# A list scheduler's cost model rewritten: turns at SBUF, durations by form, tiling changes, and new stage targets

## The chip, the cores and the metric

The kernel runs on one core of one Trainium2 chip, in one launch. The metric is device time in microseconds (us); the time before is the median of three runs. The engines are TensorE (PE, with its weight loads as PEld), VectorE (DVE), ScalarE (ACT), GpSimd (POOL) and SyncE (SP), which issues the transfers.

## The reference

The input is 32 images of 56 x 56 pixels and 96 channels, in fp32. Four layers follow each other on each image.

```python
# layer 0: conditional block. rw: four expert weights per image
rw = sigmoid(mean(x, (1, 2)) @ Wr + br)
h = relu(bn1(x @ einsum("be,ecm->bcm", rw, Wpw) + rw @ bpw))     # 96 -> 384 channels
h = relu(bn2(sum_e rw[e] * (depthwise3x3(h, Wdw[e]) + bdw[e])))
x = bn3(h @ einsum("be,emf->bmf", rw, Wpwl) + rw @ bpwl) + x     # 384 -> 96
# layer 1: x + depthwise5x5(x, kernel)
# layer 2: bn(pointwise(depthwise3x3(relu(x))))
# layer 3: shifted-window attention (7 x 7 windows, 3 heads of 32), then an MLP 96 -> 384 -> 96 with gelu,
#          layer norms ahead of both, residuals around both
```

## The kernel before, in words

The work of an image is four stages, written as Python generators. **stage_router** brings the image in as xT (96 channels by 3136 pixels), averages it on ScalarE, and mixes the experts' weights on VectorE (wmix, wmix2, mix and biases). **stage_conditional** goes through 4 strips of 14 rows by 3 blocks of 128 channels: `expand` makes h1 by a matmul and a ScalarE activation with a border of one pixel; then nine taps of the depthwise filter run over h1, the first on ScalarE, the other eight as scalar_tensor_tensor on VectorE (128 x 784 elements, output h2); `project` brings 384 channels back to 96 (y), and GpSimd adds y into xT. That makes 96 such VectorE instructions an image, 3072 in all. **stage_depthwise** does both depthwise layers as 32x32 matmuls with banded weights (band, twelve to a group, sixteen tiles of TensorE side by side), moves results by DMA (x1, x3, filtered), and makes the tokens by `filtered x pw` into res. **stage_swin** normalizes (`normalized`: square on ScalarE, sum on VectorE into var, power -0.5 and multiplication on GpSimd into lnd), turns lnd by a TensorE transpose into slots or hT, makes queries, keys and values (wq, wk, wv), scores (kT x qT), exponentials on ScalarE (exps; GpSimd masks some), denominators and averages (ones32, v), the projection wo, and the MLP (`hidden`: w1 and gelu into hid; `perceptron`: w2, and tb summed by GpSimd and VectorE and stored).

Buffers are rings of a few slots: eight PSUM banks for everything, one h1 for each of the three channel blocks, three lnd, two tb, two image buffers xT, five hid, two hT.

No instruction is issued when a stage calls it. A `Recorder` notes every call with its reads and writes and a target time; `order()` then runs a list scheduler over all notes, with a clock of its own, and `give()` issues the calls in the order found. Therefore all instructions have one line in the profile, L500, and are told apart by their tiles. Calls under `together()` stay one unit. On the chip each engine works through its instructions in that fixed order and waits on semaphores; the scheduler's clock has no part in it.

The list scheduler works as follows. Each unit has a duration from `cost()` (L165, with the table COST, L146), and a target from its stage: image number plus a start, plus a share of a length, both from PLAN (L157). Each engine has a queue sorted by target. Whenever an engine is free on the scheduler's clock, it begins the first unit in its queue whose inputs are ready and whose buffers are free. A result counts as ready for TensorE only after TO_TENSOR (L160), for another engine after CROSSING (L158); DMAs land after LANDING. A GpSimd unit and a VectorE scalar_tensor_tensor that overlap are both slowed by SHARING = 1.36. If TensorE has had nothing that it could begin for SPARE_AFTER (L161), the scheduler puts in a spare matmul of ident by ident (128x128) into a free bank. These fillers are real instructions of the program.

The recorded calls go out here:

```python
for w in self.order():
    ...
    for method, args, kw in w.calls:
        ...
        getattr(getattr(self.nc, w.engine), method)(*args, **kw)
```

A second version of the kernel for large attention scores is in the program under a branch, and is not run with this input.

Of the kernel before, what the change touches and what calls it, by code (L numbers as in the profile page):

```python
# [23 lines left out]
P = 128  # L24
# [83 lines left out]
def tile_scores_in_range(ctx: ExitStack, tc: tile.TileContext, a: dict, flag: bass.AP):  # L108
# [35 lines left out]


COST = {  # L146
    ("vector", "scalar_tensor_tensor"): (150, 1.16), ("vector", "tensor_tensor"): (180, 0.96),
    ("vector", "tensor_scalar"): (190, 0.78), ("vector", "tensor_reduce"): (180, 0.95),
    ("vector", "tensor_copy"): (180, 1.1), ("vector", "reciprocal"): (180, 6.2),
    ("scalar", "activation"): (200, 0.72), ("scalar", "copy"): (200, 0.72),  # L150
    ("gpsimd", "tensor_tensor"): (200, 2.1), ("gpsimd", "memset"): (150, 0),
    ("sync", "dma_start"): (550, 0),
}
LANDING = 3000
IMAGE_LANDING = 12000

PLAN = {"router": (-0.14, 1), "conditional": (0.72, 1.14), "depthwise": (1.48, 1.13), "swin": (3.09, 0.92)}  # L157
CROSSING = 350  # L158

TO_TENSOR = {"vector": 1500, "gpsimd": 1500, "scalar": 1000, "sync": 700}  # L160
SPARE_AFTER = 250  # L161
SHARING = 1.36


def cost(engine, method, args, kw):  # L165
    if method == "preload_act_table_set":
        return 1300
    out = kw["out"] if "out" in kw else args[0]
    n = math.prod(out.shape[1:])
    if engine == "tensor":  # L170
        if method == "transpose":
            return 127
        k, m = args[1].shape[0], math.prod(args[1].shape[1:])
        if k == 32 and m == 32:
            return 68 * n / 392
        if k == 32:
            return 86
        if m == 32:
            return 75 if n < 128 else 255
        return 195 if n < 128 else 80 + 1.6 * n  # L180
    if len(args) > 3 and args[3] == ALU.pow:
        return 200 + 200 * n
    fixed, each = COST[engine, method]
    if engine == "scalar":
        if kw.get("accum_out") is not None:
            fixed += 190
        if hasattr(kw.get("scale"), "shape"):
            each += 0.37 if hasattr(kw.get("bias"), "shape") else 0.23
        elif hasattr(kw.get("bias"), "shape"):
            each += 0.25  # L190
    return fixed + each * n


# [67 lines left out]
class Recorder:  # L261
# [30 lines left out]
    def call(self, engine, method, args, kw, reads=(), writes=()):  # L292
# [46 lines left out]
    def order(self):  # L339
# [15 lines left out]
        for w in self.work:  # L355
            for b in w.uses:
                b.left = len(b.users)
        queues = {e: [] for e in self.ENGINES}
# [16 lines left out]
        running = {}  # L375

        def share(now):

            nonlocal count
            rate = SHARING if len(running) > 1 else 1.0  # L380
            for r in running.values():
                r["left"] -= (now - r["since"]) / r["rate"]
                r["since"], r["rate"] = now, rate
                r["end"] = free[r["work"].engine] = now + max(r["left"], 0.0) * rate
                heapq.heappush(events, (r["end"], count, r))
                count += 1
# [16 lines left out]
        now = 0.0  # L403
        count = 0

        def begin(w):
            nonlocal count
            for b in w.needs:
                if b.slot is None:
                    b.ring.free.sort()  # L410
                    b.slot = b.ring.free.pop(0)[1]
                    b.ring.begun += 1
            result.append(w)
            w.start = now
# [12 lines left out]

        left = len(self.work)
        spares = 0
        begun = False  # L430
        while left:
            for e in self.ENGINES:
                if free[e] > now:
                    continue
                held = []
                while queues[e]:
                    item = heapq.heappop(queues[e])
                    w = self.work[item[1]]
                    if not available(w):
                        held.append(item)  # L440
                        continue
                    begin(w)
                    left -= 1
                    if e == "tensor":
                        spares, begun = 0, True
                    break
                else:
                    if e == "tensor" and begun and self.spare and now >= free[e] + SPARE_AFTER and self.spare[2].free:
                        lhs, rhs, ring = self.spare
                        w = Work(e, 0.0)  # L450
                        b = Buffer(ring)
                        operands = View(b, ring.tiles[0])[:, : rhs.shape[1]], lhs, rhs
                        w.calls.append(("matmul", operands, {"start": True, "stop": True}))
                        w.ns = cost(e, "matmul", operands, {})
                        w.needs, w.starts, w.uses, w.writes = [b], [b], [b], [b]
                        b.users[w], b.left, b.owner = True, 1, w
                        spares += 1
                        assert spares < 10000, "no work can start"
                        begin(w)
                for item in held:  # L460
                    heapq.heappush(queues[e], item)
            assert events, "no work can start"
            now = events[0][0]
            ready = []
            while events and events[0][0] <= now:
                _, _, w = heapq.heappop(events)
                if isinstance(w, tuple):
                    put(w[0])
                elif isinstance(w, dict):

                    if w["end"] == now and running.get(w["work"].engine) is w:
                        del running[w["work"].engine]
                        w["work"].end = now
                        done(w["work"], now)
                        share(now)
# [28 lines left out]
def kernel(  # L504
# [994 lines left out]
    def when(stage, b):  # L1499

        start, length = PLAN[stage]
        return b + start, length
# [64 lines left out]
```

## Time and profile before

| | us |
|---|---|
| median of three runs | 5206.15 |
| lowest and highest | 5203.51, 5209.27 |
| span of the profiled execution | 5212.6 |
| TensorE busy | 5050.6 |
| VectorE busy | 4300.9 |
| ScalarE busy | 3836.9 |
| GpSimd busy | 3028.8 |

The profiled execution has no time of its own beside its span, which is 6.45 us (0.12%) above the median of the runs. The page names the engines PE, PEld, DVE, ACT, POOL and SP. Its groups show a tile with what it is made from: `h<-h,mix,h` are the taps on VectorE, `banks<-x,band` the 32x32 matmuls, `banks<-ident` the fillers (1672 records, two for each fp32 matmul), `lnd<-res,var` GpSimd's multiplication in the layer norms. Mean durations of the main groups: taps 1113 ns, GpSimd's addition into xT 1838 ns, its power into var 1519 ns, its multiplication into lnd 1168 ns, gelu 582 ns. A line of waits names the waiting engine and tile, what it waited for, the sum in us, how often, and the longest. [...] The profiled core ran at a mean granted TensorE clock of 0.985.

### The profile page before, as it was taken

To read this page: it belongs to the slowest core of one execution; us is meant where nothing else is said; L and a number is where in the kernel's file an instruction comes from. 1 tells how busy PE (TensorE), PEld (TensorE's weight loads), DVE (VectorE), ACT (ScalarE), POOL (GpSimd) and SP (SyncE) were. 2 spreads that over 40 slices of the span, in tenths; PEclk is the share of its full clock that TensorE was granted. 3 is DMA by queue.
4 is the path that set the end of the run, shared out by engine and by line. 5 is a ranking of instruction groups with operands and counts; after the bars stand their busy time and mean duration, and the time that the engine had idled before them with its cause. 6 is when DMAs were issued, how large, how long until landed. Compare 5 with 4: busy or idle time off the path is not lost.

```text
span 5212.6 us, 139630 instructions
## 1 busy us (share of the span) xinstructions
PE 5050.6 (97%) x58578; PEld 3343.9 (64%) x58578; DVE 4300.9 (83%) x5561; ACT 3836.9 (74%) x7649; POOL 3028.8 (58%) x2432
## 2 busy tenths in 40 slices
PE   5789999999999999999999999999999999999999
PEld 4556666666666666666666666666666666666677
DVE  7877988888888888888888888888888888888722
ACT  3457778877778777777877777877777877777755
POOL 5455766565665556666555665656576555566533
PEclk9899999999999999999999999999999999999999
DMA  1111101111111111111111111111111111110110
GB/s 43 23 28 37 38 18 32 33 39 36 39 21 30 31 39 36 39 23 30 33 35 37 37 30 26 30 36 38 37 35 22 32 33 39 36 39 21 23 28 19
DMA packets 482577, 166.34 MB, mean 32 GB/s; under 512 B 477951, under 2 KB 478612, under 8 KB 478868
## 3 DMA queue, kind: packets, MB, share of 16 engines
q1 hardware_dynamic: 481940, 157.33, 14.8%
q8 instruction: 463, 7.59, 0.6%
q14 instruction: 174, 1.43, 0.1%
HBM read 41.60 MB, written 38.54 MB: 15 GB/s over the span
## 4 chain that ended last, share of the span: by engine, by line
PE 74%; POOL 10%; DVE 5%; ACT 5%; issue 4%; DMA 1%; SPq 0%; ACTq 0%; DVEq 0%; POOLq 0%
PE banks L500 74%; DVE h L500 3%; POOL tb L500 3%; POOL lnd L500 2%; POOL xT L500 2%; ACT exps L500 2%; POOL exps L500 2%; POOL var L500 1%; ACT hid L500 1%; ACT h L500 1%; DMA out<-tb 1%; DVE wmix L500 1%; DVE hid L500 1%; ACT slots L500 0%; DVE res L500 0%
## 5 line engine op out<-in xcount | busy, mean ns | idle before, releaser
L500 DVE SCALAR_TENSOR_TENSOR h<-h,mix,h 128x784 f32<-128x784 f32 x3072 | 3309.6, 1113 | 71.1 <-ACT h L500 54.0
L500 POOL TENSOR_TENSOR var<-var,mhalf 112x4 f32<-112x4 f32 (+1 forms) x512 | 775.2, 1519 | 426.3 <-DVE var L500 419.6
L500 PE MATMUL banks<-x,band 32*32 32x392 f32 x24576 | 856.3, 510 | 0.0
L500 POOL TENSOR_TENSOR xT<-y,xT 96x392 f32<-96x392 f32 x256 | 470.2, 1838 | 445.5 <-ACT y L500 444.1
L500 PE MATMUL banks<-xT,wmix 96*128 96x448 f32 (+1 forms) x1536 | 697.9, 553 | 0.5 <-DVE wmix L500 0.5
L500 ACT ACTIVATE h<-h,biasd,s 128x784 f32<-128x784 f32 x384 | 398.9, 1039 | 366.1 <-DVE h L500 366.0
L500 ACT ACTIVATE hid<-banks,c 128x448 f32<-128x448 f32 (+1 forms) x768 | 436.5, 582 | 288.3 <-PE banks L500 279.9
L500 POOL TENSOR_TENSOR tb<-res 112x384 f32<-112x384 f32 (+1 forms) x256 | 476.4, 1866 | 286.7 <-DMA out<-tb 196.7
L500 PEld LDWEIGHTS banks<-w,hid 128*112 128x112 f32 x5376 | 584.7, 183 | 82.0 <-issue 37.8
L500 PE MATMUL banks<-hT,w 96*128 96x448 f32 (+1 forms) x1536 | 615.6, 502 | 0.2 <-DVE tb L500 0.2
L500 POOL TENSOR_TENSOR lnd<-res,var 112x384 f32<-112x384 f32 (+1 forms) x512 | 594.8, 1168 | 32.8 <-PE banks L500 16.2
L500 ACT ACTIVATE h<-banks,bias,s 128x448 f32<-128x448 f32 (+1 forms) x768 | 538.6, 709 | 91.0 <-PE banks L500 85.4
L500 PE MATMUL banks<-w,hid 128*112 128x96 f32 x5376 | 593.1, 267 | 7.4 <-ACT hid L500 6.4
L500 PE MATMUL banks<-h,wmix 128*96 128x392 f32 x1536 | 557.7, 501 | 15.7 <-ACT h L500 15.7
L500 PEld LDWEIGHTS banks<-x,band 32*32 32x32 f32 x24576 | 404.7, 103 | 250.9 <-issue 165.9
L500 ACT ACTIVATE exps<-banks 49x196 f32<-49x196 f32 x1536 | 506.2, 330 | 40.2 <-PE banks L500 15.3
L500 POOL TENSOR_TENSOR exps<-exps,keep_column 49x147 f32<-49x147 f32 x224 | 207.1, 925 | 480.8 <-ACT exps L500 427.4
L500 PEld LDWEIGHTS banks<-h,wmix 128*96 128x96 f32 x1536 | 244.1, 165 | 256.8 <-issue 209.2
L500 PEld LDWEIGHTS banks<-xT,wmix 96*128 96x128 f32 x1536 | 261.2, 192 | 200.7 <-issue 95.5
L500 DVE TENSOR_REDUCE var<-lnsq 112x4 f32<-112x388 f32 (+1 forms) x512 | 253.1, 497 | 157.6 <-POOL lnd L500 118.1
L500 ACT ACTIVATE h<-h,mix 128x784 f32<-128x784 f32 x384 | 364.5, 949 | 18.0 <-POOL h L500 10.1
L500 PEld LDWEIGHTS banks<-hT,w 96*128 96x128 f32 x1536 | 256.4, 190 | 144.9 <-issue 74.8
(132 smaller groups left out, 7460.2 us busy)
## 6 DMA issues: line engine op xcount, KB each, us to landing
xT<-in_x SPq DMA_DIRECT2D x32, 1176.0 KB
x<-xT SPq DMA_DIRECT2D x384, 98.0 KB
out<-tb SPq DMA_DIRECT2D x128, 168.0 KB
filtered<-x SPq DMA_DIRECT2D x384, 49.0 KB
filtered<-x SPq DMA_DIRECT2D x384, 42.0 KB
out<-tb SPq DMA_DIRECT2D x128, 126.0 KB
filtered<-x SPq DMA_DIRECT2D x384, 7.0 KB
wpw<-in_L_conv_Wpw SPq DMA_DIRECT2D x1, 576.0 KB
```

Of the source, the lines that this page charges most:

```text
L500: getattr(getattr(self.nc, w.engine), method)(*args, **kw)
```

## The change

Only the scheduler's model and its constants change; the stages and what they compute stay as they are.

- **Durations.** COST gets new values for nearly every form. VectorE's tensor_reduce is priced by its input, not its output. GpSimd's tensor_tensor goes from 200 + 2.1 n to 230 + 1.5 n ns for n elements, its power from 200 + 200 n to 370 + 160 n. A DMA issue takes SP 120 instead of 550 ns.
- **TensorE.** `tensor_time()` prices a unit by its columns and by how many tiles work side by side. A unit whose `tiling()` (rows and columns rounded up to 32, 64 or 128) differs from the one before costs CHANGE = 170 ns more. Code to prefer units of the same tiling is added, and switched off by SAME = 0.
- **Turns at SBUF.** Instead of slowing both by 1.36, a tensor_tensor or scalar_tensor_tensor of VectorE or GpSimd that touches no PSUM holds a single port for its whole duration (`in_memory`, `port`); the next one begins after it, in the order in which the scheduler reached them.
- **AHEAD.** An engine takes its next unit 37 to 100 ns before the end of the last.
- **Latencies and fillers.** CROSSING 350 to 522; TO_TENSOR lower for every engine; SPARE_AFTER 250 to 459.
- **Targets.** PLAN is set anew: the router starts 0.36 of an image earlier, the depthwise stage 0.05 later and shorter; the conditional stage is nearly and the attention stage exactly as before.
- **available()** refuses a unit that uses a buffer which has no slot yet and which another unit begins.

```diff
 COST = {
...
-    ("gpsimd", "tensor_tensor"): (200, 2.1), ("gpsimd", "memset"): (150, 0),
-    ("sync", "dma_start"): (550, 0),
+    ("vector", "scalar_tensor_tensor"): (155, 1.11), ("vector", "tensor_tensor"): (150, 1.02),
+    ("vector", "tensor_scalar"): (150, 1.04), ("vector", "tensor_reduce"): (145, 1.02),
...
+    ("gpsimd", "tensor_tensor"): (230, 1.5), ("gpsimd", "memset"): (145, 0),
+    ("sync", "dma_start"): (120, 0),
 }
+AHEAD = {"vector": 77, "scalar": 100, "gpsimd": 37, "tensor": 0, "sync": 0}
...
-PLAN = {"router": (-0.14, 1), "conditional": (0.72, 1.14), "depthwise": (1.48, 1.13), "swin": (3.09, 0.92)}
-CROSSING = 350
-
-TO_TENSOR = {"vector": 1500, "gpsimd": 1500, "scalar": 1000, "sync": 700}
-SPARE_AFTER = 250
-SHARING = 1.36
+PLAN = {"router": (-0.499, 0.953), "conditional": (0.712, 1.141), "depthwise": (1.529, 1.103), "swin": (3.09, 0.92)}
+CROSSING = 522
+
+TO_TENSOR = {"vector": 1155, "gpsimd": 1362, "scalar": 778, "sync": 136}
+SPARE_AFTER = 459
+CHANGE = 170
+SAME = 0
+
+def up(n):
+    return 32 if n <= 32 else 64 if n <= 64 else 128
+
+def tiling(call):
+    return tuple(up(n) for n in call[1][1].shape[:1] + (math.prod(call[1][1].shape[1:]),))
+
+def tensor_time(calls):
+    rows, columns = tiling(calls[0])
+    beside = min(len(calls), (P // rows) * (P // columns))
+    if beside == 16 and len(calls) % 16:
+        beside = 12
+    total = 30 if beside > 1 else 0
+    for method, args, kw in calls:
+        m = math.prod(args[1].shape[1:])
+        n = args[1].shape[0] if method == "transpose" else math.prod(args[2].shape[1:])
+        total += 2 * ((max(n, m) if beside == 1 else n) / 1.2 + 5) / beside
+    return total
+
+def in_memory(w):
+    method, args, kw = w.calls[0]
+    return method in ("tensor_tensor", "scalar_tensor_tensor") and not any(
+        isinstance(v, View) and v.buffer.ring.banks for v in args
+    )
...
         def available(w):
+            if any(b.slot is None and b.owner is not w and b not in w.needs for b in w.uses):
+                return False
...
-            if e == "gpsimd" or e == "vector" and w.calls[0][0] == "scalar_tensor_tensor":
-                running[e] = {"work": w, "left": w.ns, "since": now, "rate": 1.0}
-                share(now)
-                return
-            free[e] = now + w.ns
+            ns = w.ns
+            if e == "tensor":
+                if w.tiling != last[0]:
+                    ns += CHANGE
+                last[0] = w.tiling
+            begun_at = now
+            if w.in_memory:
+                begun_at = max(now, port[0])
+                port[0] = begun_at + ns
+            free[e] = begun_at + ns - AHEAD[e]
             heapq.heappush(events, (free[e], count, None))
-            heapq.heappush(events, (free[e] + w.landing, count + 1, w))
+            heapq.heappush(events, (begun_at + ns + w.landing, count + 1, w))
```

More of the change, by code (lines that the diff above doesn't have):

```diff
@@ L146 @@
 COST = {
[L147 to L150, printed above, removed]
-    ("gpsimd", "tensor_tensor"): (200, 2.1), ("gpsimd", "memset"): (150, 0),
-    ("sync", "dma_start"): (550, 0),
+    ("vector", "scalar_tensor_tensor"): (155, 1.11), ("vector", "tensor_tensor"): (150, 1.02),
@@ L153 @@
+    ("vector", "tensor_scalar"): (150, 1.04), ("vector", "tensor_reduce"): (145, 1.02),
+    ("vector", "tensor_copy"): (150, 1.04), ("vector", "reciprocal"): (150, 6.2),
+    ("scalar", "activation"): (210, 0.72), ("scalar", "copy"): (210, 0.7),
+    ("gpsimd", "tensor_tensor"): (230, 1.5), ("gpsimd", "memset"): (145, 0),
+    ("sync", "dma_start"): (120, 0),
 }
+AHEAD = {"vector": 77, "scalar": 100, "gpsimd": 37, "tensor": 0, "sync": 0}
 LANDING = 3000
 IMAGE_LANDING = 12000
-PLAN = {"router": (-0.14, 1), "conditional": (0.72, 1.14), "depthwise": (1.48, 1.13), "swin": (3.09, 0.92)}
@@ L165, in cost @@
 def cost(engine, method, args, kw):
+    if engine == "tensor":
+        return 0
     if method == "preload_act_table_set":
@@ L169, in cost @@
     n = math.prod(out.shape[1:])
[L170 to L180, printed above, removed]
     if len(args) > 3 and args[3] == ALU.pow:
-        return 200 + 200 * n
+        return 370 + 160 * n
     fixed, each = COST[engine, method]
+    if method == "tensor_reduce":
+        n = math.prod(args[1].shape[1:])
     if engine == "scalar":
@@ L187, in cost @@
         if hasattr(kw.get("scale"), "shape"):
-            each += 0.37 if hasattr(kw.get("bias"), "shape") else 0.23
+            each += 0.32 if hasattr(kw.get("bias"), "shape") else 0.21
         elif hasattr(kw.get("bias"), "shape"):
-            each += 0.25
+            each += 0.2
     return fixed + each * n
@@ L357, in order @@
                 b.left = len(b.users)
+            w.in_memory = w.engine in ("vector", "gpsimd") and in_memory(w)
+            if w.engine == "tensor":
+                w.tiling, w.ns = tiling(w.calls[0]), tensor_time(w.calls)
+        port, last = [0.0], [None]
         queues = {e: [] for e in self.ENGINES}
@@ L373, in available @@
             )
[L375 to L386, printed above, removed]
         def done(w, now):
@@ L435, in order @@
                 held = []
+                first = None
                 while queues[e]:
@@ L441, in order @@
                         continue
+                    if e == "tensor" and SAME:
+                        if first is None:
+                            first = item
+                        if item[0] > first[0] + SAME:
+                            held.append(item)
+                            w = None
+                        elif w.tiling != last[0]:
+                            held.append(item)
+                            continue
+                        if w is None:
+                            break
                     begin(w)
@@ L445, in order @@
                         spares, begun = 0, True
+                    first = None
                     break
-                else:
+                if first is not None:
+                    held.remove(first)
+                    begin(self.work[first[1]])
+                    left -= 1
+                    spares, begun = 0, True
+                elif free[e] <= now:
                     if e == "tensor" and begun and self.spare and now >= free[e] + SPARE_AFTER and self.spare[2].free:
@@ L453, in order @@
                         w.calls.append(("matmul", operands, {"start": True, "stop": True}))
-                        w.ns = cost(e, "matmul", operands, {})
+                        w.tiling, w.ns = tiling(w.calls[0]), tensor_time(w.calls)
+                        w.in_memory = False
                         w.needs, w.starts, w.uses, w.writes = [b], [b], [b], [b]
@@ L468, in order @@
                     put(w[0])
[L469 to L475, printed above, removed]
                 elif w is not None:
```

## The prediction

> **What bounds the kernel now.** I read the page's busy shares and slices first, then windows cut where the first, fourth and last conditional stage ends, then TensorE's waits, the chain of waits, and the two queues behind the longest wait.
>
> ```profile
> PE 5050.6 (97%) x58578; PEld 3343.9 (64%) x58578; DVE 4300.9 (83%) x5561; ACT 3836.9 (74%) x7649; POOL 3028.8 (58%) x2432
> ...
> PE   5789999999999999999999999999999999999999
> ...
> DVE  7877988888888888888888888888888888888722
> ```
>
> TensorE is near full from the fourth slice to the end. The windows (span, then busy time of each engine) split the run at 586.1 us, where the fourth image's last tap on VectorE ends, and at 4928.0 us, where the last image's does:
>
> ```profile
> 0.00:586.10 586.10, 486.01 (x4952) 325.41 (x4953) 474.06 (x643) 332.05 (x601) 334.04 (x194) 0.94 0.14 30
> 586.10:4928.00 4341.90, 4287.06 (x50357) 2802.72 (x50355) 3765.86 (x4801) 3345.62 (x6685) 2588.60 (x2101) 0.99 0.16 33
> 4928.00:5212.60 284.60, 277.52 (x3275) 215.80 (x3273) 61.02 (x120) 159.20 (x364) 106.16 (x139) 1.00 0.12 25
> ```
>
> So there is a ramp of 586.1 us, 28 images at 4341.9/28 = 155.07 us, and a tail of 284.6 us. In the middle TensorE idles 4341.9 - 4287.1 = 54.8 us, 1.96 us an image. What it waits for, over the whole run:
>
> ```profile
> PE banks L500 <- POOL lnd L500: 51.3, 45, 2.8
> PE banks L500 <- ACT h L500: 47.4, 16, 5.4
> ```
>
> The second line lies before 400 us. The first is the middle's, and comes back with every second image. The chain of waits around one such place, then GpSimd's and VectorE's queues there:
>
> ```profile
> 1199.05 5.80 issue
> 1204.84 4.86 POOL lnd L500
> 1209.70 0.04 issue
> 1209.74 30.30 PE banks L500 x243
> ```
>
> ```profile
> 1198.96 5.90 POOL L500 TENSOR_TENSOR var<-var,mhalf 112x3 f32<-112x3 f32 x1
> ...
> 1205.14 3.86 DVE L500 SCALAR_TENSOR_TENSOR h<-h,mix,h 128x784 f32<-128x784 f32 x4
> ```
>
> GpSimd's power of 112x3 takes 5.90 us here against a mean of 1448 ns, and the multiplication behind it 4.86 us against 1340 ns, while VectorE's taps run without a gap. At its worst the 112x288 addition into tb takes as long as ten taps:
>
> ```profile
> 1081.12 9.64 POOL L500 TENSOR_TENSOR tb<-res 112x288 f32<-112x288 f32 x1 [2.38 <-DMA out<-tb]
> ...
> 1080.70 9.54 DVE L500 SCALAR_TENSOR_TENSOR h<-h,mix,h 128x784 f32<-128x784 f32 x10
> ```
>
> [...] above, GpSimd stood behind ten taps. [...] from the starts of matmuls in the trace, a change costs some 0.40 us after a 32x32 group, 0.34 after the 113x32 group of 392 columns, 0.16 after the other two small forms, 0.10 out of the full array. [...] I count instructions and waits, and use 97% only to say who is waited for.
>
> **The change, part by part.** No computation is added or dropped. The same 5,664 groups of real matmuls, the same taps and DMAs are put in another order, and the number of fillers differs (a filler is the 128x128 matmul of ident that the list inserts where it believes TensorE idle). I compared the two orders engine by engine.
>
> *Tiling changes.* 1808 before, 1840 after. With the four prices above they come to 356.2 and 355.9 us: fewer changes out of 32x32 groups (468 to 387), more out of the 113x32 group (31 to 117). The new price makes the list's clock right, but with SAME = 0 nothing groups equal tilings. Cost: 0; bounds -5 and +5 (32 x 0.16).
>
> *Fillers.* 836 to 856. A filler is two records; in the timeline at 296.6 us eleven records take 1.39 us with the last one's own 0.275, so they follow each other at 0.112 us and a filler takes 0.224 (the group's mean, 242.5/836 = 0.29 us, is the upper end, as many stand alone). Where they stand matters: up to the fourth conditional's end 384 before, 265 after; in the middle 281 and 504; in the tail 171 and 87. In the middle TensorE is the bound, so 223 more cost 223 x 0.224 = **+50 us**. They cost as little as +15 if most fall where TensorE would wait anyhow, and +65 at 0.29.
>
> *Ramp.* VectorE sets it: 474 of 586 us. The taps keep their order; the new order puts some 12 us more of VectorE's other work and 26 us more of TensorE's ahead of the third conditional's end, and 15 us more of TensorE's ahead of the fourth's (group means, scaled by 0.855, since the groups' sum of 5685 us overlaps and the true total without fillers is 5050 - 187 = 4863 us). Twelve us later at the third, then 10 us less matmul work and 21 x 0.224 = 5 us fewer fillers up to the fourth: **-3 us**, bounds -20 and +12.
>
> *Tail.* After the last tap, 290 us of real matmuls (group means) are left before, 273 after: 17 x 0.855 = -14 us. Of the 84 fillers dropped (19 us) I take half, for some stand in real gaps: **-24 us**, bounds -33 and -10. What moved ahead makes the middle no longer: its real matmuls change by -1.5 us and -2 us of tiling changes, **-3.5 us**.
>
> *Turns at SBUF.* Old list: both engines slowed by 1.36 when together. New: strict turns. VectorE's runs of taps and like instructions without another form between get shorter: runs of 11, 12, 14 and 17 once in two images before, none above 8 after. So the waits of 5 to 10 us should shrink, and with them lnd's 48 us of the middle. Against that stand tighter places. In matmul time between producer and consumer in the list, under 2.5 us: lnd to its transpose 2.0 an image before, 3.8 after; hT to w1's matmul 0.4 and 5.4; hid to w2's 7.5 and 10.9; GpSimd's exps 4.1 and 0.7; oT 4.9 and 2.3. An hT takes ScalarE 0.71 us and queues behind other activations. I take 40 us of lnd's wait gone and 8 us of new waits: **-32 us**. Bounds: -50 (all gone) and +60 (a wait of the 1.15 us that lnd has now, 51.3/45, at two more places an image).
>
> *Other edits.* DMA issues priced 120 instead of 550 ns, latencies, the routers' and depthwise stages' earlier or later targets: the number of DMAs on SP's queue stays, and the 16 DMA engines are at most 0.16 busy in these windows. The router starts a third of an image earlier, but its image buffer has two slots and its wait cost TensorE 11.8 us in all. They are hidden by TensorE's other matmuls: 0. If that cover went, the 11.8 us is what it could cost. The stricter test in available() touches only which work may start.
>
> **Sum** against the profiled 5212.6 us: -3 + 50 - 3.5 - 24 - 32 = -12.5. The median of the runs, 5206.15, stands 6.45 us below the span; I carry the difference over: 5206.15 - 12.5 = **5194 us**.
>
> **Rivals.**
> *A. The fillers are paid and GpSimd stays behind the taps.* Place: lnd's multiplication ahead of its transpose, and hT ahead of w1. For it: 3.8 tight lnd instead of 2.0, five taps in a row suffice for the 5.90 us above, and the list still trusts in a turn after one tap. Against: the shorter runs. With no wait saved and the tail at -14: -3 + 50 - 3.5 - 14 = +29.5, **5236 us**. It decides from where the middle's waits fall by less than 50 - 30.5 = 19.5 us, 0.7 us an image.
> *B. The fillers fall into real gaps.* Then they cost 15, all of lnd's wait goes, the tail gives -30: -3 + 15 - 3.5 - 30 - 45 = -66, **5140 us**. Against: in this trace the middle has only 2 us of gaps an image to fill, and 8 more fillers need 1.8.
> *C. No difference.* The planner's model moves only the list's clock; tiling changes cost the same, TensorE has the same real work, and waits saved equal fillers added: **5206 us**. This is also the case in which the count of tilings doesn't do what it says.
>
> **How the numbers follow.** Forecast 0.40, of which 0.10 falls within 0.2% of 5206 (10 us, about what a measurement of this kernel can tell from no change); B 0.16; C 0.08; A 0.36. Faster by more than 0.2%: 0.30 + 0.16 = 0.46; within: 0.10 + 0.08 = 0.18; slower: 0.36. The forecast alone runs from 5172 to 5212 (its bounds of ramp and tail). For 8 in 10 the range goes to 5155, half-way to B, and to 5250, beyond A by half of the upper bound of new waits.
>
> **What would show it.** Right: fillers of 1712 records; in the middle lnd's wait below 10 us and TensorE's idle below 1 us an image; 28 images at about 155.5 us; a tail near 260 us; no GpSimd addition above 8 us. Wrong: a middle of 157 us or more an image with waits for lnd or hT at its head (A), or one below 154 (B). A ramp above 600 us would make the third term wrong.

## The result: 7.3% slower, and the profile after

The changed kernel takes 5581.68 us (median of 4 runs, 5575.91 to 5605.46), the kernel before 5206.23 beside it: ratio 1.073, 95% interval 1.0708 to 1.0752. The profiled execution is the slowest of the four, 5605.46 us with a span of 5603.7, so the profile shows 391 us more span where the medians differ by 375.

The page after, busy time by engine and three rows of slices:

```profile
PE 5285.3 (94%) x58618; PEld 3546.8 (63%) x58618; DVE 4237.3 (76%) x5561; ACT 3886.1 (69%) x7649; POOL 3250.4 (58%) x2432
...
PE   5788999999999999999999999999999999999999
...
DVE  7967787777788777787777877778888777877632
...
PEclk8899999999999999999999999999999999999999
```

TensorE issues 40 instructions more than before and is busy 234.7 us longer; VectorE, with the same instructions, is busy 64 us less. Its slices are mostly 7, not 8. The windows, cut at the end of the fourth and the last conditional stage (span, busy time of PE, PEld, DVE, ACT, POOL, then granted clock, DMA share, GB/s):

```profile
0.00:597.30 597.30, 472.92 (x4886) 306.57 (x4886) 471.63 (x646) 336.02 (x610) 335.39 (x197) 0.91 0.14 30
597.30:5347.50 4750.20, 4565.55 (x50843) 3055.51 (x50840) 3705.23 (x4800) 3395.23 (x6687) 2812.93 (x2103) 0.94 0.14 30
5347.50:5603.70 256.20, 246.84 (x2916) 184.70 (x2892) 60.43 (x118) 154.80 (x354) 102.07 (x134) 0.99 0.12 26
```

All of the loss is in the middle: 4750.2 us for 28 images, 169.65 an image where it was 155.07. The ramp is 11.2 us longer, the tail 28.4 us shorter. Two numbers of the middle moved. TensorE's idle time went from 54.8 to 184.7 us, and its mean granted clock from 0.99 to 0.94. By the trace's clock records, the time in the middle in which the granted clock was one half ("half clock" below) went from 81.9 to 600.7 us. What TensorE waits for in the middle (sum, times, longest, us):

```profile
PE banks L535 <- POOL lnd L535: 184.0, 56, 4.9
```

It is the line that was to shrink. In every one of the 28 images there is one gap of 4.85 to 4.92 us ahead of four transposes of lnd, 136.2 us in all; no other gap of the middle is over 2 us. The timeline of GpSimd, VectorE and TensorE around one of them (start, us, then the idle time before and who ended it in brackets):

```profile
2161.11 5.52 POOL L535 TENSOR_TENSOR var<-var,mhalf 112x4 f32<-112x4 f32 x1 [5.53 <-DVE var L535]
2166.72 2.93 POOL L535 TENSOR_TENSOR lnd<-res,var 112x384 f32<-112x384 f32 x1
...
2160.49 0.54 DVE L535 TENSOR_REDUCE var<-lnsq 112x4 f32<-112x388 f32 x1
2160.96 4.80 DVE L535 SCALAR_TENSOR_TENSOR h<-h,mix,h 128x784 f32<-128x784 f32 x5
2165.68 0.44 DVE L535 TENSOR_REDUCE var<-lnsq 112x3 f32<-112x291 f32 x1
2166.05 2.91 DVE L535 SCALAR_TENSOR_TENSOR h<-h,mix,h 128x784 f32<-128x784 f32 x3
...
2160.73 4.11 PE L535 MATMUL banks<-h,wmix 128*96 128x392 f32 x12
2169.70 0.98 PE L535 MATMUL banks<-ident,lnd 112*96 112x112 f32 x4 [4.86 <-POOL lnd L535]
```

Read it from the top. VectorE's reduction of the first attention row ends at 2161.03, and GpSimd's power begins at once. It lasts until after VectorE's five taps (elsewhere the same power takes 1.0 us); the multiplication behind it lasts until after the next three (elsewhere 0.82 us). TensorE has run out of `project` matmuls at 2164.84 and waits for 4.86 us. In the list only two taps lie between this multiplication and its transposes, and TensorE's units there are priced at 2.0 us in all. Then come three windows, the columns as above:

```profile
2160.00:2170.00 10.00, 5.14 (x18) 2.51 (x17) 9.28 (x12) 4.55 (x7) 8.81 (x3) 0.96 0.55 100
2170.00:2190.00 20.00, 20.00 (x120) 15.61 (x123) 11.71 (x13) 10.81 (x24) 9.04 (x9) 0.51 0.21 52
2190.00:2200.00 10.00, 10.00 (x368) 7.80 (x362) 8.45 (x12) 5.38 (x8) 5.57 (x3) 1.00 0.02 4
```

For 20 us after the gap TensorE is busy all the time, at a granted clock of 0.51. So a wait of 4.86 us has a second price: 20.5 us at half clock in 22 of the 28 images, 23.9 us in three (in the other three, after a gap of the same length, 3.4 to 6.8 us). If work at half clock takes twice as long, the middle's sum is +129.9 (idle) + (600.7 - 81.9)/2 = 259.4 (clock) + 50 (fillers, as predicted) - 3.5 = 435.8 us, against 408.3 measured; it is 27 us too high. e1 and e13 below, with the same order and little half clock, put that down to the clock's term: by them the 600.7 us cost some 272 us, not 300, in part because 17.5 of them fall into idle time. So the clock's share of the loss is some 235 us, and 259 is its upper end.

The theory to test: **the new list puts the transposes of the first row so close behind GpSimd's multiplication that GpSimd, standing behind taps without a gap, is late in every image; the gap halves the clock, in most images for 20 us.** Rivals: the 223 fillers cost the time; the new targets or the turns put other stages in each other's way; GpSimd is late through its own queue.

### The profile page after: what moved, and what is told of

Same layout as the page of the kernel before. It is cut to its first block, busy times and chain, and to the rows that moved or that the text cites. A ratio compares the mean times of both kernels' runs of the same rounds, so it can differ in the third digit from the quotient of the medians.

```text
span 5603.7 us, 139492 instructions
## 1 busy us (share of the span) xinstructions
PE 5285.3 (94%) x58618; PEld 3546.8 (63%) x58618; DVE 4237.3 (76%) x5561; ACT 3886.1 (69%) x7649; POOL 3250.4 (58%) x2432
## 4 chain that ended last, share of the span: by engine, by line
PE 54%; POOL 25%; issue 11%; DVE 5%; ACT 3%; DMA 2%; SPq 0%; POOLq 0%; ACTq 0%; DVEq 0%
PE banks L535 54%; POOL var L535 8%; POOL lnd L535 6%; POOL tb L535 5%; DVE h L535 4%; POOL xT L535 3%; POOL exps L535 3%; DMA out<-tb 1%; ACT h L535 1%; ACT exps L535 1%; ACT hid L535 0%; ACT y L535 0%; DVE tb L535 0%; ACT lnsq L535 0%; DMA wpwl<-in_L_conv_Wpwl 0%
## 5 line engine op out<-in xcount | busy, mean ns | idle before, releaser
L535 DVE SCALAR_TENSOR_TENSOR h<-h,mix,h 128x784 f32<-128x784 f32 x3072 | 3264.9, 1105 | 80.3 <-ACT h L535 74.5
L535 POOL TENSOR_TENSOR var<-var,mhalf 112x4 f32<-112x4 f32 (+1 forms) x512 | 992.9, 1941 | 629.4 <-DVE var L535 610.1
L535 POOL TENSOR_TENSOR lnd<-res,var 112x384 f32<-112x384 f32 (+1 forms) x512 | 681.1, 1331 | 510.3 <-PE banks L535 493.2
L535 PE MATMUL banks<-xT,wmix 96*128 96x448 f32 (+1 forms) x1536 | 737.8, 576 | 27.6 <-ACT h L535 26.6
L535 POOL TENSOR_TENSOR xT<-y,xT 96x392 f32<-96x392 f32 x256 | 446.9, 1750 | 266.3 <-ACT y L535 200.7
L535 PEld LDWEIGHTS banks<-x,band 32*32 32x32 f32 x24576 | 432.9, 104 | 245.0 <-issue 103.5
L535 POOL TENSOR_TENSOR tb<-res 112x384 f32<-112x384 f32 (+1 forms) x256 | 445.3, 1748 | 165.9 <-DMA out<-tb 56.9
L535 PE MATMUL banks<-ident,lnd 112*96 112x112 f32 x1792 | 280.3, 276 | 199.5 <-POOL lnd L535 199.5
L535 POOL TENSOR_TENSOR exps<-exps,keep_column 49x147 f32<-49x147 f32 x224 | 139.9, 625 | 538.2 <-ACT exps L535 428.1
L535 PEld LDWEIGHTS banks<-ident,lnd 112*96 112x96 f32 x1792 | 200.6, 135 | 346.0 <-POOL lnd L535 243.5
```

## The experiments

Times stand beside those of the kernel before on the same chip. e1 to e12 are single executions; half clock, idle time and gaps of TensorE are of the middle, from the trace. "Allowance" is TO_TENSOR for GpSimd: the lag from a GpSimd result to the TensorE unit that reads it, on the list's clock.

**e1_fill: keep the order, fill the gap.**

```diff
+                for _ in range(w.fill):   # 22 for turn1(0)'s transposes, else 0
+                    bank = w.calls[0][1][0].buffer
+                    self.nc.tensor.matmul(bank.ring.tiles[bank.slot][:, :P], self.spare[0], self.spare[1], start=True, stop=True)   # ident, ident
```

> The changed kernel in exactly its order, with 22 more fillers (matmuls of ident by ident into the bank that the transposes then overwrite, 22 x 0.224 = 4.9 us) right ahead of the transposes of the first row's lnd in each image's attention stage, where TensorE stood idle for some 4.9 us an image. Theory 'clock': the idle gap makes the granted clock fall to one half for some 20 us after it, so about 10 us an image are lost beside the gap itself; with the gap filled the clock stays up, and the time falls by 28 x 10 = 280 us to about 5300, with the half-clock time of the middle (600 us in the changed kernel's trace) below 150. Rival 'pace': GpSimd's chain of powers and multiplications sets the period of 170 us by itself and TensorE merely waits for it; then the fillers change the time by less than 1%, 5530 to 5640, since a faster TensorE only waits longer. Rival 'fillers': fillers are paid in full; then it is slower by 32 x 4.9 = 158 us, 5740.

5365.48 us (before 5203.46). The middle of e1:

```profile
595.30:5097.80 4502.50, 4449.19 (x52073) 3014.06 (x52072) 3713.18 (x4800) 3393.38 (x6687) 2829.30 (x2103) 1.00 0.15 32
```

Half clock falls from 600.7 to 37.5 us, and no gap over 2 us is left. In the middle 616 fillers (138 us at 0.224) took the place of 131 us of idle time, and still it is 4750.2 - 4502.5 = 248 us shorter. That is the clock's part, some 60% of the middle's loss. The time is 65 us above the 5300 expected by the theory, and far from what its rivals expected (5530 to 5640, and 5740).

**e2_old_plan, e3_allow, e4_no_turns: one term of the model at a time.** e2 puts the old PLAN back, e3 raises the allowance, e4 takes the turns out:

```diff
-PLAN = {"router": (-0.499, 0.953), "conditional": (0.712, 1.141), "depthwise": (1.529, 1.103), "swin": (3.09, 0.92)}
+PLAN = {"router": (-0.14, 1), "conditional": (0.72, 1.14), "depthwise": (1.48, 1.13), "swin": (3.09, 0.92)}
--- e3
-TO_TENSOR = {"vector": 1155, "gpsimd": 1362, "scalar": 778, "sync": 136}
+TO_TENSOR = {"vector": 1155, "gpsimd": 5000, "scalar": 778, "sync": 136}
--- e4
-            if w.in_memory:
-                begun_at = max(now, port[0])
-                port[0] = begun_at + ns
```

> The changed kernel with the stage targets (PLAN) of the kernel before, all else new. If the new targets make the place at which the first row's lnd is late, the middle goes back to about 155 us an image and the time to 5200 to 5280. If the model of strict turns at SBUF makes it (it lets the list put GpSimd's units where on the chip they stand behind runs of taps), lnd waits stay, at this row or another, and the time stays above 5400.

> The changed kernel with one constant changed: a GpSimd result counts as ready for TensorE only after 5000 instead of 1362 ns, so that every lnd is placed some 3.6 us further ahead of its transposes. Theory 'clock' (one late lnd an image costs its gap and then a halved clock): the wait for lnd falls from 199.5 us to below 60, the half-clock time of the middle below 200 us, and the time to 5200 to 5330. Rival 'pace' (GpSimd's throughput behind the taps sets the period): the wait moves to other tiles and the time stays within 2% of 5582.

> The changed kernel without the turns at SBUF in the list's clock: GpSimd and VectorE units are priced alone and never hold each other up there (the rest of the change stays). The list then believes in GpSimd results earlier than the chip gives them, while it puts in far fewer fillers (337 instead of 856) and 1996 tiling changes. If the strict turns were the harmful part, 5150 to 5250. If the harm is that lists trust GpSimd too much in any form, lnd and exps waits grow: above 5582.[...]

e2 5427.89, e3 5207.72, e4 5611.01 us. One number of the table takes away the whole loss. The middle of e3, and its wait for lnd over the whole run:

```profile
582.20:4927.20 4345.00, 4312.53 (x50991) 2890.84 (x50991) 3724.47 (x4799) 3353.67 (x6681) 3016.01 (x2103) 1.00 0.15 33
```

```profile
PE banks L535 <- POOL lnd L535: 16.8, 18, 1.6
```

Half clock is 3.4 us, idle 32.5. Yet GpSimd isn't blocked less on the whole: between 1000 and 4500 us, 68 of its operations before, 151 after and 172 in e3 took over 2 us more than the fastest with the same tiles. At the first row two things differ. The list leaves four or five taps in turn (4.6 or 5.7 us of TensorE's units) between its multiplication and its transposes instead of two (2.0 us), and the pair itself stands elsewhere and is hardly held up:

```profile
2166.05 1.75 POOL L535 TENSOR_TENSOR var<-var,mhalf 112x4 f32<-112x4 f32 x1
2167.88 0.83 POOL L535 TENSOR_TENSOR lnd<-res,var 112x384 f32<-112x384 f32 x1
```

e3 alone doesn't tell the two apart; e8 to e10 below do. e2 and e4 give orders with late places of their own: in e2 TensorE waits 82.2 us for lnd and 72.4 for ScalarE's h (half clock 256 us), in e4 70.4 us for GpSimd's exps and 55.8 for lnd (563 us).

**e5_again: the kernel before, its order untouched, with only the first row's multiplication made late.**

```diff
-                for method, args, kw in w.calls:
+                for method, args, kw in w.calls * w.again:   # 9 for norm1(0)'s multiplication, else 1
```

> The kernel before in its own order, with GpSimd's multiplication into the first row's lnd of each image's attention stage done nine times instead of once (same operands, same values; eight more at 0.82 us alone, some 6.6 to 10 us of delay on GpSimd's queue). Theory 'clock': TensorE, which stood idle in gaps of at most 2.8 us, now meets a gap above 4 us in most images, and each is followed by some 20 us of half clock; the time grows by more than the gaps themselves, by 28 x (about 4 to 6 us of gap + 10 us) = 390 to 450 us to about 5600 to 5650, with 500 us or more of half clock in the middle. If the halved clock in the changed kernel has another cause[...], the time grows by the gaps only, 110 to 170 us, and half-clock time stays near 82 us. If GpSimd has slack enough at this row, nothing changes (5206).

5753.75 us (before 5208.27): 545 us, 17.0 an image, for eight more multiplications, which alone would take 8 x 0.82 = 6.6 us. That is above the expected 5600 to 5650. Lnd's wait in the middle is 287.3 us, half clock 675.8, idle 371.8. Lateness at this one place is enough to lose as much, in the old order too. Here the waiting itself is the greater part: idle time grew by 317 us, and 217 of the 675.8 us at half clock fall into it.

**e6_allow_no_fill and e7_before_no_fill: what the fillers cost.** e3 and the kernel before, with the fillers that the list puts after 600 us of its clock left out at issue, all else in order:

```diff
+                if w.filler and w.start > 600000.0:
+                    continue
```

> The kernel with the 5000 ns allowance, in the same order, but without the 675 fillers that its list puts in after 600 us of its own clock (they are left out at issue, nothing else moves). If fillers in the middle are paid, as the prediction had it, up to 675 x 0.224 = 151 us are saved: 5055 to 5090. If they stand in time in which TensorE would wait anyhow, 5190 to 5206. If they are what keeps the clock up, gaps above 4 us appear with half-clock time behind them: slower than 5206.

> The kernel before in the same order without its 452 fillers after 600 us of the list's clock. Paid fillers: 452 x 0.224 = 101 us saved at most, 5100 to 5130. Fillers in real gaps: 5190 to 5206. Fillers needed by the clock: above 5206, with more than 82 us of half clock in the middle.

e6 5233.74, e7 5209.18 us (before 5208.27). Without its 579 fillers of the middle e3's order is 26 us slower: idle goes from 32.5 to 126.4 us, half clock from 3.4 to 85.3. Without its 281, and 171 in the tail, the kernel before takes the same time, from two parts: the middle is 12 us longer (idle 54.8 to 98.6, half clock 81.9 to 143.4), the tail 18.8 us shorter (284.6 to 265.8). The price of a filler was right (middle less idle less half of the half-clock time falls by 62.6/281 = 0.223 us for each in e7, by 112.0/579 = 0.193 in e6). That the middle gets shorter by it without them is wrong: most stand where TensorE would idle (43.8 of the 62.6 us and 93.9 of the 112.0 turn into idle time), and they keep the clock up. In the tail about half of their price is paid.

**e8_old_pool and e10_first_row: can the place alone be mended?** e8 puts GpSimd's old durations back; e10 gives 3638 ns more to the first row's multiplication only (1362 + 3638 = 5000):

```diff
-    ("gpsimd", "tensor_tensor"): (230, 1.5), ("gpsimd", "memset"): (145, 0),
+    ("gpsimd", "tensor_tensor"): (200, 2.1), ("gpsimd", "memset"): (145, 0),
-        return 370 + 160 * n
+        return 200 + 200 * n
--- e10
-... TO_TENSOR[w.engine] if v.engine == "tensor" ...
+... TO_TENSOR[w.engine] + w.extra if v.engine == "tensor" ...   # extra 3638 for norm1(0)'s multiplication, else 0
```

> The changed kernel with only GpSimd's two old prices back (200 + 2.1 n, power 200 + 200 n; these are 1.2 to 1.4 times the lone durations and so leave room for standing behind a tap). If it is the cut of these prices to lone durations that puts lnd too near its transposes, the lnd wait falls below 60 us and half-clock time of the middle below 200 us; the list then also puts in 340 more fillers in the middle (76 us), so 5250 to 5330. If the prices are not what matters, the late lnd stays and the time is above 5450.

> The changed kernel with the 5000 ns allowance for one single GpSimd unit of each image, the multiplication into lnd of the attention stage's first row; all other GpSimd results keep 1362. If the late first row is the whole story, this does nearly what 5000 for all does: no gaps above 4 us, below 150 us of half clock, 5200 to 5290. If the lists' other tight places (five more transposes with two taps ahead of them) matter as much, they take over: above 5400.

e8 5508.80 us (before 5208.27), e10 5436.06 (before 5209.51). Both still have the pair of 5.5 and 2.93 us ahead of transposes, with 15 gaps over 3.5 us in e8 (one every second image) and 26 in e10 (3.5 and 4.3 us in turn). In e8 the pair is held up alike in every image, and the gap follows the list: 4.9 us where TensorE's units between the multiplication and its transposes are priced at 2.2 us, 1.0 us where at 5.3. Two images in a row:

```profile
2311.34 0.59 PE L535 MATMUL banks<-ident,lnd 112*96 112x112 f32 x4 [1.05 <-POOL lnd L535]
...
2472.04 0.98 PE L535 MATMUL banks<-ident,lnd 112*96 112x112 f32 x4 [4.90 <-POOL lnd L535]
```

In e10 the list leaves four taps (3.3 us), as many as e3 does in every second image, and TensorE still waits, for here the pair stands behind eight taps as before. So the gap is what the lateness exceeds TensorE's remaining work by, and both sides count.

**e9_allow_3000, e12_allow_8000, e11_before_allow: is 5000 a rule?** The allowance at 3000 and 8000 in the changed kernel, and 1500 to 5000 in the kernel before:

```diff
--- e9, e12
-TO_TENSOR = {"vector": 1155, "gpsimd": 1362, "scalar": 778, "sync": 136}
+TO_TENSOR = {"vector": 1155, "gpsimd": 3000, "scalar": 778, "sync": 136}   # e12: 8000
--- e11
-TO_TENSOR = {"vector": 1500, "gpsimd": 1500, "scalar": 1000, "sync": 700}
+TO_TENSOR = {"vector": 1500, "gpsimd": 5000, "scalar": 1000, "sync": 700}
```

> The changed kernel with GpSimd results ready for TensorE after 3000 ns on the list's clock (1362 in the changed kernel: 5582 us; 5000: 5208 us). In its list three taps stand between the first row's multiplication into lnd and its transposes (two in the changed kernel, five with 5000). If room ahead of the transposes is what counts, it lies between: gaps of some 2 to 4 us at the first row, 100 to 400 us of half clock, 5250 to 5450. If any other property of the order with 5000 made it fast, it may be anywhere, above 5500 as well.

> The changed kernel with 8000 ns for GpSimd results on the way to TensorE. With 5000 the waits for lnd in the middle are already small (16.8 us in the whole run) and the middle's clock is full, so nothing is left to gain there: 5190 to 5240 by the theory that only late GpSimd results matter. If the period with 5000 is still set by GpSimd's queue, it falls below 5180.

> The kernel before (old model, old targets) with 5000 instead of 1500 ns for GpSimd results on the way to TensorE. If the allowance is good for any list here, the 48 us of waits for lnd in the middle go, and the half clock behind them (82 us, so 41 us of work): 5110 to 5190. If the old list's period of 155 us has other causes (its waits are only where TensorE has time to spare), 5190 to 5220. If the longer allowance costs more in placing than it saves, above 5220.

e9 5218.67, e12 5290.50, e11 5404.28 us (before 5209.51). e9 is faster and e12 slower than anything expected of them. With 3000 the first row has three taps ahead of its transposes (3.4 us); its power takes 1.75 us, its multiplication 4.62 us behind taps, and TensorE has no gap over 2 us. With 8000 lnd is no longer waited for; oT (27.2 us), hT (22.9), res and hid are late instead. In the old model 5000 costs 195 us. TensorE's waits there, over the whole run:

```profile
PE banks L500 <- POOL lnd L500: 54.1, 18, 9.0
PE banks L500 <- POOL exps L500: 52.3, 16, 6.3
```

The waits for lnd are fewer but longer (before, 45 of at most 2.8 us), and those for GpSimd's exps are new in the middle. So 5000 goes with the new model's other numbers and is no figure of the chip.

**e13_breaks: the changed kernel, its order untouched, with a way in for GpSimd.** After each of the first five taps that follow the first row's reduction, VectorE makes a short reduction of a weight (one input), whose result isn't used:

```diff
+                if w.engine == "vector":
+                    if w.breaks:             # 5 on norm1(0)'s reduction, else 0
+                        due = w.breaks
+                    elif due and w.calls[0][0] == "scalar_tensor_tensor":
+                        due -= 1
+                        self.nc.vector.tensor_reduce(*self.pause, AX.X, ALU.add)   # pause, w2 (128x288)
```

> The changed kernel in its own order, with five VectorE reductions more an image: one (w2's 128x288, one SBUF input, about 0.44 us, result unused) after each of the first five taps that follow the reduction of the first attention row. Nothing on GpSimd's or TensorE's queue moves. Theory (GpSimd stands behind gapless taps, the late transposes idle TensorE for 4.9 us, and the granted clock is then half for 20 us): the first row's power falls from 5.5 us to 2 us or less, its multiplication from 2.9 to 2 or less, TensorE's gap ahead of the transposes from 4.9 to under 2 us, half clock in the middle from 601 us to under 200, time 5230 to 5350 us. Rival (GpSimd is late through its own queue or its inputs, the taps beside it are a coincidence): both keep their durations, the gap stays above 4 us and the time above 5540 us. Third case (the gap goes but the clock stays halved, so the gap was not its cause): gap under 2 us, half clock above 400 us, time 5400 to 5500 us.

5254.25 us (2 runs), ratio to before 1.0087 (1.0057 to 1.0116). The same place in its timeline:

```profile
2047.19 1.74 POOL L537 TENSOR_TENSOR var<-var,mhalf 112x4 f32<-112x4 f32 x1 [4.58 <-DVE var L537]
2049.01 1.03 POOL L537 TENSOR_TENSOR lnd<-res,var 112x384 f32<-112x384 f32 x1
...
2046.57 0.54 DVE L537 TENSOR_REDUCE var<-lnsq 112x4 f32<-112x388 f32 x1
2047.03 1.02 DVE L537 SCALAR_TENSOR_TENSOR h<-h,mix,h 128x784 f32<-128x784 f32 x1
2047.98 0.44 DVE L543 TENSOR_REDUCE pause<-w 128x1 f32<-128x288 f32 x1
2048.34 1.02 DVE L537 SCALAR_TENSOR_TENSOR h<-h,mix,h 128x784 f32<-128x784 f32 x1
2049.28 0.44 DVE L543 TENSOR_REDUCE pause<-w 128x1 f32<-128x288 f32 x1
...
2046.75 4.11 PE L537 MATMUL banks<-h,wmix 128*96 128x392 f32 x12
2050.70 0.55 PE L537 MATMUL banks<-ident,lnd 112*96 112x112 f32 x4
```

The power is let in by the first break: 1.74 us instead of 5.52. The multiplication is let in by the second: 1.03 instead of 2.93. The transposes follow `project` without idle time. Half clock is 34.1 us, no gap is over 2 us, and 5 x 0.44 = 2.2 us more VectorE work an image has brought back 327 of 375 us. Nothing but the breaks differs from the changed kernel, so GpSimd's own queue is no cause. What is left against before lies in the middle (+57.7 us: idle +34, half of the half clock -24, the rest +47) and the ramp (+10), less a tail 28 us shorter.

**e14_all_breaks, e15_before_breaks, e16_before_breaks_no_fill: breaks everywhere.** Two breaks behind each of the 16 layer-norm reductions of an image, in e6, in the kernel before, and in e7:

```diff
-    def normalized(src, n):
+    def normalized(src, n, breaks=2):
```

> The changed kernel with the allowance for GpSimd at 5000 ns and without fillers in the middle (as e6_allow_no_fill, 5234 us), plus two such reductions after the first two taps that follow each of the 16 reductions of a layer norm an image: about 32 x 0.44 = 14 us of VectorE an image, which has about 22 us an image to spare. If waits behind taps are what keeps the period at 155 us: TensorE's idle in the middle falls from 126 us to under 60, time 5150 to 5200 us. If VectorE has no room, or taps late for the projection are next: idle stays or rises, time 5230 to 5350 us.

> The kernel before, its order and fillers as they are, plus the same two reductions after the first two taps behind each of the 16 layer norm reductions an image (14 us of VectorE an image). If GpSimd's waits behind taps cost the kernel before its 55 us of idle and 82 us of half clock in the middle: idle under 30, half clock under 40, time 5150 to 5190 us. If they cost it little, since its list leaves room, and VectorE's added work moves other stages: 5206 us or more, up to 5300.

> As e15, without the 281 fillers in the middle. If the breaks close the gaps in which the fillers stood: 10 to 60 us below e15's time (281 x 0.224 = 63 us at most). If the gaps are others (VectorE's taps, ScalarE's activations): same as e15 within 20 us, with TensorE's idle higher by the fillers' time.

e14 5228.95 us (ratio 1.0036, 1.0016 to 1.0055), not clear of e6's single 5233.74; e15 5280.08 (1.0136, 1.0107 to 1.0166), e16 5338.93 (1.0249, 1.022 to 1.0279). e15's operations of GpSimd that are over 2 us late fall from 68 to 36, and it is 72 us slower: idle 54.8 to 105.0. Where the list leaves room, a long wait behind taps costs nothing, and 14 us more of VectorE an image do cost. For e16 both expectations were wrong: without fillers it is 59 us slower than e15, half clock 286.7 instead of 95.6 us. Here the fillers are needed.

**e17_allow_to_96 and e18_allow_to_200: the good middle with the short tail.** e3, with the allowance back at 1362 once only 96 or 200 of VectorE's scalar_tensor_tensor are left:

```diff
-... TO_TENSOR[w.engine] if v.engine == "tensor" ...
+... (TO_TENSOR[w.engine] if w.engine != "gpsimd" or taps[0] > 96 else 1362) if v.engine == "tensor" ...
```

> As e3_allow (allowance for GpSimd 5000 ns, 5208 us), but back to 1362 ns once only 96 of VectorE's scalar_tensor_tensor are left to begin, so for the last image or so. The list up to there is the same, and 14 us less of TensorE's work by the list's own prices (its durations and tiling changes left aside) lies behind the last tap. If room is needed only against taps: ramp and middle as in e3_allow (582 and 4345 us), tail 256 to 268 instead of 278.7 us, time 5185 to 5200 us. If the work that leaves the tail comes back as waits ahead of the last tap: middle longer by as much, time 5203 to 5213 us.

> The same with 200 left instead of 96, so from the last two images on. If room is needed only against taps, one image more in the tight order brings 4.9 us of gap and 10 us of half clock once or twice: 5 to 20 us above e17's time. If the tail alone decides: the same as e17 within 5 us.

e17 5194.41 us (10 runs, 5191.69 to 5197.96), ratio to the kernel before 0.9974 (0.9965 to 0.9984); e18 5194.06 (12 runs), 0.9978 (0.9969 to 0.9986). e17's windows:

```profile
0.00:584.80 584.80, 473.36 (x4813) 301.18 (x4813) 469.50 (x646) 336.68 (x610) 314.92 (x195) 0.93 0.14 31
584.80:4935.70 4350.90, 4316.58 (x51031) 2889.61 (x51029) 3724.14 (x4799) 3361.64 (x6687) 3014.55 (x2105) 1.00 0.15 33
4935.70:5194.90 259.20, 247.62 (x2921) 184.69 (x2916) 60.89 (x117) 154.23 (x352) 102.62 (x134) 1.00 0.12 26
```

The tail is 259.2 us, against 278.7 in e3 and 284.6 before; the middle stays near e3's. Both versions are faster than the kernel before by 0.2 to 0.3%. e18 has one gap over 3.5 us in the middle where e17 has none, and doesn't pay for it measurably: the 5 to 20 us expected for it didn't come.

## Why the prediction was wrong

The forecast was 5194 us, the range ended at 5250, and the kernel took 5581.68.

**Turns at SBUF, -32 us (bounds -50 and +60): the step that failed**, by direction and by size. Idle time rose by 129.9 us, and half clock added some 235 us. Three readings led there.

First, the working took long runs of taps for the danger and counted runs above 8. The new list has indeed none of them, and the longest addition into tb fell from 9.64 to 5.62 us, as "no GpSimd addition above 8 us" said. But five taps were enough, and the number of blocked operations more than doubled. What decides, beside the lateness, is how much of TensorE's work the list has between a blocked result and the unit that needs it (e8, e10). The prediction had that count (lnd to its transpose under 2.5 us in the list: 2.0 an image before, 3.8 after) and valued a new tight place at 1.15 us, the mean of the old waits. It was 4.86 us: one tight place in every image where power and multiplication both stand behind taps.

Second, the place shown as the middle's wait wasn't it. The chain at 1204.84 cost TensorE 0.24 us. 38.5 of the 47.5 us that the middle waited for lnd were 14 gaps of 2.75 us, and there the multiplication isn't slow itself; an addition into tb ahead of it in GpSimd's queue stands behind five taps:

```profile
1209.74 0.59 PE L500 MATMUL banks<-ident,lnd 112*96 112x112 f32 x4 [0.24 <-POOL lnd L500]
...
1068.54 5.03 POOL L500 TENSOR_TENSOR tb<-res 112x288 f32<-112x288 f32 x1
1074.50 0.66 POOL L500 TENSOR_TENSOR lnd<-res,var 112x288 f32<-112x288 f32 x1
...
1075.21 0.49 PE L500 MATMUL banks<-ident,lnd 112*96 112x112 f32 x3 [2.75 <-POOL lnd L500]
```

Third, a wait was priced at its own length. The clock didn't enter the sum. The windows of before already showed 0.99 in the middle, and the trace 14 stretches at half clock there, one at each gap of 2.75 us, 81.9 us in all, 5.85 us for each. So the trace of before already showed that a wait could not be priced by its length; in that of after a gap of 4.9 us is followed by 20.5 us at half clock in 22 of the 28 images.

**Rival A** had the mechanism and the place: GpSimd stays behind the taps, and lnd is late ahead of its transpose. Its price, no wait saved and none added, was 5236 us. The missing 345 us are the longer wait and the clock. The sign it gave, a middle over 157 us an image with waits for lnd, came out at 169.65.

**Fillers, +50 us.** The count was right (1712 records) and 0.224 us each too. As busy time the term holds: e13, in the changed order and nearly without half clock, has a middle that, less idle time and half of its half clock, is 47 us above before's, where fillers and middle work were put at 46.5. As a cost of its own it doesn't: e6 and e7 show that leaving them out makes the middle no shorter. Rival B's premise, that they fall into gaps, was the better one for the middle; its hope that lnd's waits go was not. In the tail, half of their price, as the prediction took it, is what e7 shows.

**Range.** Its ends don't follow from their working: the bounds of ramp and tail add up to 5168 and 5223, not 5172 and 5212, and rival A with half of 60 us is 5266, not 5250. None of these reaches 5581.68.

**Ramp, -3 us:** +11.2, just within its bounds. **Tail, -24 us:** -28.4, right. **Tiling changes 0 and middle work -3.5 us:** not measured one by one; with fillers, idle time and half of the half clock taken off, the middle is 4198.8 us in e6 and 4183.6 in e7, 15 us apart, so that nothing large hides there. **Other edits, 0:** e2 is 154 us faster than the changed kernel with the old targets alone, so the targets do decide where the stages meet; they were not free, in this order.

Open is which edit of the diff brings the first row so close and puts its pair behind eight taps. Going back on targets (e2), turns (e4) or GpSimd's durations (e8) alone leaves 5428 to 5611 us. The new values of CROSSING and AHEAD, the TensorE prices and the 138 ns less allowance weren't tried alone.

## What to carry to other kernels

A model of contention that grants turns promises results which the chip doesn't always deliver (here a power took 5.52 us behind five taps, 1.0 elsewhere); ask of each result that may be blocked how much work the consumer's engine has left before it must wait. Price a wait of TensorE with the half clock that its trace shows behind it (here 20.5 us or more behind a gap of 4.9 in 25 of 28 images), and look at the granted clock of each window before adding up busy times (the middle's was 0.94 here, 0.99 before). A filler where TensorE would wait anyhow wasn't a cost here (without its 281 fillers the middle of e7 was 12 us longer). Room in a list wasn't free either: 8000 instead of 5000 ns cost 83 us here, and in the tail, where no taps are left, less room was better (259.2 us in e17, 278.7 in e3).

## What the runs showed of the hardware

**Gaps and the clock.** Over the middles of the twenty traces: of gaps of 2 to 3.5 us, 164 of 189 have a stretch at half clock beginning within 6 us before or 8 us after their end, 5 to 8 us long in the mean; of gaps of 3.5 to 6 us, 109 of 109, and from 4.5 us on the stretch is 17 to 19 us in the mean. Of gaps of 1 to 2 us it is 170 of 461; of moments taken at random, about one in ten. One long gap isn't needed: in e4 290 of the 563 us at half clock, and in e16 225 of the 287, lie in stretches without a gap of 2 us in the 6.8 us before them. In the middle of the kernel before, 4 stretches were 3.4 us long and 10 were 6.8; in that of the changed kernel 21 were 3.4, one 6.8, 22 were 20.5 and three 23.9. Each of these 25 long ones began 0.4 to 0.9 us before the end of its gap, and TensorE had no idle time in the rest of it. Why it is 20 us and more in 25 images and 3.4 to 6.8 us in three isn't known.

**GpSimd behind VectorE.** Between taps that follow each other without a gap, GpSimd often doesn't get its turn after the first: a power of 112x4 stood 5.52 us behind five of them. It is not a rule. In the middle of the changed kernel, of 335 GpSimd operations that began beside a tap with at least two more close behind, 167 were done as soon as their own length after that tap allows, within 0.25 us, and 168 stood to the end of the run; what decides between the two isn't known. The other way round, a tap in e3 took 4.08 us (1.02 alone) while GpSimd ran four operations without a gap. In e13, with a reduction of 0.44 us with one input behind the first tap, the power took 1.74 us, not 5.52. Counted alike over the middles of the twenty traces, a waiting GpSimd operation was let in at 4993 of 5057 of VectorE's reductions, but between two taps only 6421 times of 16055.
